# Moving work units between the turns of a transformer block: turns 0, 2, 3 and 25, and the last pair spread out

## The chip, the cores and the metric

The kernel runs on one core of one Trainium2 chip. The metric is the device time of one execution in microseconds (us). Before the change the median of three runs was 1411.21 us (1409.51 to 1415.54). A profile shows one further execution.

## The reference

The input x holds 8 batches of 512 tokens of width 256. The block computes, all in float32:

```python
x = x + attn(layernorm(x))            # attention, then a 3-tap convolution of its
                                      # context gives new queries: a second attention
                                      # with the same k and v, then out_w
x = x + ffn(layernorm(x))             # where ffn is itself:
#   h = x + attention(rmsnorm(x, g1)) # third attention, q and k rotated (rope)
#   y = h + moe(rmsnorm(h, g2))       # top 2 of 8 experts, hidden width 704
```

Each attention has 16 heads of width 16 and a causal mask. So there are three attentions for each batch, and behind them a router and a mixture of experts over all 4096 tokens.

## The kernel before, in words

**Two stages.** First come the attentions of all batches, with every projection around them; each token's normed row is written to a table in DRAM (`xtab`), grouped by expert. Then the experts run over tiles of 384 rows of that table (`expert_tile`, L814) and add their results to `out` by indirect DMA.

**Pairs and turns.** Batches are handled in pairs, called pair 0 to pair 3 here. In the code `one` and `two` are the batches of a pair, `before0` and `before1` those of the pair before it, `next0` and `next1` those of the pair after it. A pair's six attentions (first of one, first of two, second of one, and so on) have 9 steps each. A step (L1283 to L1312) is: score matmuls for 4 heads into two PSUM tiles `sc` (there are two such buffers in all), two ACT instructions `pr<-sc` that take the exponentials (L1297), and one POOL instruction that masks the diagonal (L1305). The products with the values (`av`, L1220) follow later, from a list called `behind`. Two steps make a turn, so a pair has 27 turns, numbered 0 to 26; the code writes them `t + n`.

**The order inside a turn** is written out by hand (loop at L1978): the score matmuls of the first step; the `av` products that are due; the mid slot (first `follow_up("mid")`, then `small_units`, then `first_units`); the score matmuls of the second step; `follow_up("late")`; the end slot (`units`, then `follow_up("end")`). "Mid" and "end" below mean these two slots. Engines take their instructions in exactly this order: the code is inside `tc.manual_schedule` for PE, ACT, DVE and POOL (L1898). SP, which issues most DMAs, runs in the order of the calls too.

**Units.** The other work is cut into units, methods of `Batch`, and `plan(turn, batch, method, arguments, among=...)` (L1762) puts each into a turn: `among=first_units` or `small_units` for the mid slot, else the end slot. A turn whose end slot has matmul units is in the set `busy`, and this decides how many `av` products it takes. Units that matter here: `transpose` (8 PE transposes of the normed x), `k`, `q`, `values` (projections, two halves each), `conv` (four parts), `h` (output projection of the third attention: 4 matmuls into one PSUM bank, a DVE addition L1622 into `rows`, a POOL addition, then two ACT squares L1625 that read `rows`), `rms` (normalises `rows`, stores x), `transpose3`, `logits`, `logits_back`, `route` (some 20 short DVE instructions with one ACT exponential among them), `slots` (2 matmuls and 18 short DVE instructions).

**PSUM banks.** Two banks, `mm0` and `mm1`, serve all units in turn (`mm_tile`, L1069). A unit's matmuls wait until the last reader of their bank is done.

**The ends of an attention's half.** `normalise` (L1230) copies sums on ACT, moves them by DMA, and queues `finish` (two DVE reciprocals of about 1.74 us, L1250, and two multiplications) and, for the first attention, `differences` (four DVE instructions, L1471 to L1474, that `conv` reads), to the mid slot of the next turn for the first half of the heads and to the end slot for the second half.

**The start.** `load_x(0)` fetches batch 0 in one DMA; PE runs 34 transposes of the identity meanwhile (L1906); DVE takes the moments, POOL the power, DVE the normed rows; then PE transposes them, ACT copies them out, and the first projections follow.

## Time and profile before

The profiled execution took 1413.67 us; its span, from the first to the last instruction on the core, is 1411.9 us, so 1.8 us lie around it. It is 2.46 us above the median of the three runs.

| stage (us from the span's start) | length, us | PE busy, us |
|---|---|---|
| start, 0 to 17.69 | 17.69 | 13.66 |
| pair 0, 17.69 to 224.08 | 206.39 | 201.26 |
| pair 1, 224.08 to 433.10 | 209.02 | 203.52 |
| pair 2, 433.10 to 647.85 | 214.75 | 206.79 |
| pair 3 and its end, 647.85 to 851.90 | 204.05 | 199.40 |
| rest of the experts, 851.90 to 1402.00 | 550.10 | 544.33 |
| end, 1402.00 to 1411.90 | 9.90 | 0.00 |

A turn is measured from its first score matmul to the next turn's first one. Lengths of the turns that the change touches, in us:

| turn | pair 0 | pair 1 | pair 2 | pair 3 |
|---|---|---|---|---|
| 0 | 9.43 | 8.55 | 8.55 | 8.55 |
| 2 | 6.14 | 8.98 | 8.99 | 8.48 |
| 3 | 8.74 | 8.62 | 8.86 | 8.61 |
| 4 | 9.40 | 8.82 | 8.82 | 8.82 |
| 5 | 6.23 | 7.86 | 11.92 | 5.39 |
| 6 | 6.21 | 6.79 | 6.79 | 6.28 |
| 7 | 8.44 | 8.36 | 8.36 | 8.85 |
| 10 to 14 | 34.22 | 34.88 | 34.65 | 32.32 |
| 22 to 24 | 21.50 | 21.50 | 21.49 | 24.83 |
| 25 | 9.78 | 9.77 | 9.77 | 5.90 |

Inside a turn the stretches are read the same way: from the first instruction of one group on PE to the first of the next. Where nothing delays them, the score matmuls of a step take 1.10 us (1.07 us for the steps of one block), a `k` or `q` unit 1.91 us, a `values` half 1.90 us, a `conv` part 1.92 us, an `h` half 1.92 us (1.82 us for the first of two in a row), and two transposed tiles 1.0 to 1.3 us. How to read the page: "idle before" names the instruction that ended an engine's wait; a busy PE is not PE at full rate, since score matmuls that have only one of the two `sc` buffers run two heads at a time and then take about 2.0 us for a step instead of 1.10.

### The profile page before, as it was taken

The page shows a single profiled execution, that of the slowest core. Times are in us where ns is not written, and L with a number is a line of the kernel's source. Part 1 is how long each engine was busy: PE and PEld are TensorE (multiplying, and loading weights), DVE is VectorE, ACT ScalarE, POOL GpSimd, SP SyncE. Part 2 cuts the span into 40 slices and gives each one's busy share as a digit, 9 for nine tenths or more (in the row PEclk, how much of TensorE's full clock was granted, in tenths as well). Part 3 has the DMA queues.
Part 4 walks back from the last instruction along what each step waited for, and adds up shares of the span by engine and source line. Part 5 has one row for each costly group of instructions (what it writes and reads, how often), then busy time and mean ns, then how long its engine had stood idle before and what let it go on. Part 6 is the DMA issues. An engine that isn't in the chain of part 4 may idle for free.

```text
span 1411.9 us, 31919 instructions
## 1 busy us (share of the span) xinstructions
PE 1369.0 (97%) x13476; PEld 892.3 (63%) x13476; DVE 739.6 (52%) x1470; ACT 723.6 (51%) x1175; POOL 525.2 (37%) x525
## 2 busy tenths in 40 slices
PE   8999999999999899999999999999999999999997
PEld 5566555566555566556565566666767677776775
DVE  5754886775887665886666865322222212222221
ACT  4677777776786677777776784321111211111120
POOL 3334434547333546433555444232122121222212
PEclk9999999999999999999999999999999999999998
DMA  5122122211001211011222022334141323232311
GB/s 151 59 82 86 66 82 77 73 40 62 13 25 53 73 40 55 20 45 39 83 72 79 21 84 71 90 81 102 23 102 31 96 32 95 46 87 42 88 26 14
DMA packets 66408, 88.42 MB, mean 63 GB/s; under 512 B 12752, under 2 KB 46736, under 8 KB 66256
## 3 DMA queue, kind: packets, MB, share of 16 engines
q1 hardware_dynamic: 52976, 68.94, 14.7%
q0 software_dynamic: 13280, 17.35, 7.0%
q8 instruction: 107, 1.75, 0.5%
q14 instruction: 45, 0.37, 0.1%
HBM read 36.35 MB, written 31.82 MB: 48 GB/s over the span
## 4 chain that ended last, share of the span: by engine, by line
PE 59%; DVE 5%; ACT 4%; DMA 1%; issue 1%; POOL 1%; DVEq 0%; POOLq 0%; ACTq 0%; SPq 0%
PE pgu L835 23%; PE po L860 13%; PE sc L1290 8%; PE av L1220 5%; PE mm L1130 3%; ACT pr L1297 2%; PE mm L1483 2%; PE mm L1119 1%; PE mm L1148 1%; PE mm L824 1%; DVE r L1250 1%; DVE c L1251 1%; PE mm L1372 1%; DMA r<-cs 1%; DMA cs<-cs 0%
## 5 line engine op out<-in xcount | busy, mean ns | idle before, releaser
L1297 ACT ACTIVATE pr<-sc 128x1024 f32<-128x1024 f32 x432 | 418.8, 1023 | 145.1 <-PE sc L1290 144.6
L1305 POOL TENSOR_TENSOR pr<-pr,seen 128x512 f32<-128x512 f32 (+1 forms) x216 | 256.6, 1188 | 395.7 <-ACT pr L1297 386.2
L835 PE MATMUL pgu<-xgT,gu 128*128 128x384 f32 (+1 forms) x1056 | 337.0, 478 | 1.9 <-DVE hT L850 1.6
L835 PEld LDWEIGHTS pgu<-xgT,gu 128*128 128x128 f32 x1056 | 200.4, 190 | 128.3 <-DVE hT L850 2.2
L849 ACT ACTIVATE sg<-pgu 128x384 f32<-128x384 f32 (+1 forms) x120 | 57.7, 481 | 404.5 <-PE pgu L835 404.4
L872 POOL DMA_INDIRECT out_dram<-share,xg x72 | 111.0, 1542 | 373.8 <-DVE share L867 299.6
L1220 PE MATMUL av<-pr,va 64*32 64x512 f32 (+7 forms) x6144 | 216.3, 407 | 0.0
L1290 PE MATMUL sc<-qT,kT 32*128 32x320 f32 (+7 forms) x2048 | 192.2, 436 | 4.3 <-ACT pr L1297 4.2
L850 DVE TENSOR_TENSOR hT<-sg,pgu 128x384 f32<-128x384 f32 (+1 forms) x120 | 65.0, 543 | 240.3 <-ACT sg L849 240.3
L860 PE MATMUL po<-dn,hT 128*128 128x256 f32 (+1 forms) x864 | 190.8, 379 | 0.0
L1220 PEld LDWEIGHTS av<-pr,va 64*32 64x32 f32 x6144 | 112.1, 106 | 101.2 <-issue 73.5
L860 PEld LDWEIGHTS po<-dn,hT 128*128 128x128 f32 (+1 forms) x864 | 159.9, 187 | 23.9
L1250 DVE RECIPROCAL r<-r 128x256 f32<-128x256 f32 x96 | 167.4, 1744 | 11.8 <-DMA r<-cs 11.7
L1290 PEld LDWEIGHTS sc<-qT,kT 32*128 32x128 f32 x2048 | 115.7, 185 | 78.3 <-ACT pr L1297 32.0
L867 DVE TENSOR_SCALAR share<-po,xg 128x256 f32<-128x256 f32 (+1 forms) x72 | 34.8, 483 | 148.6 <-PE po L860 148.5
L1290 PE MATMUL sc<-q2T,kT 32*128 32x512 f32 (+7 forms) x1024 | 93.0, 434 | 0.6 <-ACT pr L1297 0.5
L1730 POOL DMA_INDIRECT xtab<-rows,slot x64 | 64.0, 1000 | 46.0 <-DVE pick L1719 29.0
L1290 PEld LDWEIGHTS sc<-q2T,kT 32*128 32x128 f32 x1024 | 58.3, 184 | 32.7 <-issue 14.5
L1130 PE MATMUL mm<-xT,wqkv_sb 128*128 128x512 f32 x128 | 63.7, 624 | 3.9 <-ACT mm L1625 2.3
L1130 PE MATMUL mm<-xaT,wqkv_sb 128*128 128x512 f32 x128 | 61.3, 612 | 2.0 <-DVE xaT L1378 2.0
L1483 PE MATMUL mm<-terms,conv_sb 128*128 128x256 f32 x256 | 62.7, 390 | 0.0
L1237 ACT ACTIVATE cs<-av 128x512 f32<-128x512 f32 x96 | 56.6, 604 | 3.7 <-PE av L1220 3.2
(181 smaller groups left out, 1305.5 us busy)
## 6 DMA issues: line engine op xcount, KB each, us to landing
r<-cs SPq DMA_DIRECT2D x96, 128.0 KB, 2.0
xtab<-pad SPq DMA_DIRECT2D x24, 397.5 KB, 3.3
xg<-xtab SPq DMA_DIRECT2D x16, 397.5 KB, 3.0
gu<-in_wg_dram SPq DMA_DIRECT2D x18, 352.0 KB, 3.1
cs<-cs SPq DMA_DIRECT2D x48, 128.0 KB, 2.0
dn<-in_wd_dram SPq DMA_DIRECT2D x9, 640.0 KB, 5.1
gu<-in_wu_dram SPq DMA_DIRECT2D x18, 320.0 KB, 3.8
x<-in_x_dram SPq DMA_DIRECT2D x8, 512.0 KB, 4.3
```

The costliest lines, as they stand in the source:

```text
L835: nc.tensor.matmul(ps, gu[d][:, n0 : n0 + P], xgT[:, d, :], start=(d == 0), stop=(d == DC - 1),)
L850: nc.vector.tensor_mul(hT[k], sg, pu)
L860: nc.tensor.matmul(po, hT[k][:, s * P : s * P + m], dn[:, k, :], start=(k == 0), stop=(k == NK - 1),)
L872: nc.gpsimd.indirect_dma_start(out=out, out_offset=token_of(xg, s, m), in_=share[:m, s, :], in_offset=None, bounds_check=B * S - 1, oob_is ...
L1130: nc.tensor.matmul(ps, w[:, d, n0 : n0 + P], srcT[:, d, :S], start=(d == 0), stop=(d == DC - 1),)
L1220: nc.tensor.matmul(av[i][g * HP : (g + 1) * HP, j * KB :], v[rows, j, ch * G + g, :], pr[rows, g, at : at + n], start=(j == 0), stop=(j == ...
L1250: nc.vector.reciprocal(r[:, half], r[:, half])
L1290: nc.tensor.matmul(sc[:, g - g0, at : at + S - j * KB], kT[r0 : r0 + HP, ch, j], qT[r0 : r0 + HP, ch, j * KB : S], start=True, stop=True,)
L1297: nc.scalar.activation(pr[:, g0 : g0 + 2], sc, AF.Exp, scale=SCALE)
L1305: nc.gpsimd.tensor_tensor(diag, diag, seen.unsqueeze(1).unsqueeze(1).to_broadcast([P, G, len(parts), KB]), ALU.mult,).ins
L1483: nc.tensor.matmul(ps[:, i], conv_sb[:, d, k, ch * P : (ch + 1) * P], self.terms[d][:, k], start=(d == 0), stop=(d == DC - 1),)
L1730: nc.gpsimd.indirect_dma_start(out=xtab, out_offset=bass.IndirectOffsetOnAxis(ap=slot[:, c, k : k + 1], axis=0), in_=rows[:, c, :], in_off ...
```

## The change

Nothing is computed differently. Each unit named still runs once. The order changes in these places:

- **Start.** Batch 0 is fetched in two DMAs and its moments, powers and normed rows are taken in two halves. The bias column `bqk_sb` is fetched ahead of the weights. The bias product moves behind the normed rows. The 8 transposes go half by half into both banks, and ACT and DVE each copy one bank out. The moments of batch 1 come after that. 22 instead of 34 transposes of the identity run ahead.
- **Rope tables (pair 0).** The four `table` units move from the end of turns 3 and 4 to the mid slots of turns 2, 3, 4 and 5.
- **Turn 0.** `q 0` of batch two moves from the end slot, between the transposes and the logits, to the mid slot.
- **Turn 2.** The first `h` half moves to the mid slot, where it stands behind `route`. **Turn 3.** `slots` moves to the mid slot. **Turn 25.** The transposes of the next pair's second batch move to the mid slot.
- **Differences** always go to the end slot.
- **Squares.** The squares of `h` are written to an SBUF tile, no longer over the PSUM bank that they came from.
- **Last pair.** `q 1`, `k 1`, `values 1`, `h 1`, `rms`, `transpose3`, the `conv` parts of both batches, `slots` and `values2 0` get turns of their own, one unit to a slot, from turn 2 to turn 23. Turn 10 thereby leaves `busy`.
- **Bias additions** on POOL move to earlier turns.

```diff
--- before.py
+++ after.py
...
     xs = {}
-    def load_x(b):
+    def load_x(b, parts=1):
         if b < B:
             xs[b] = keep.tile([P, NC, D], F32, tag="x", name="x", bufs=4)
-            nc.sync.dma_start(xs[b], x[b * S : (b + 1) * S, :].rearrange("(c p) d -> p c d", p=P))
+            of = x[b * S : (b + 1) * S, :].rearrange("(c p) d -> p c d", p=P)
+            n = NC // parts
+            for c in range(0, NC, n):
+                nc.sync.dma_start(xs[b][:, c : c + n, :], of[:, c : c + n, :])
...
-    load_x(0)
+    load_x(0, 2)
...
+        bqk_sb = column(bqkv[: 2 * D], 2 * D, "bqk_sb")
         wqkv_sb = weight(wqkvT, 3 * D, "wqkv_sb")
-        bqk_sb = column(bqkv[: 2 * D], 2 * D, "bqk_sb")
...
-
         bk_sb = wp.tile([P, DC, 2], F32, tag="bk", name="bk_sb")
-        for ch in range(DC):
-            nc.vector.tensor_scalar(
-                bk_sb[:, ch, :], parity, bqk_sb[:, DC + ch : DC + ch + 1], None, ALU.mult
-            )
+
+        def bias_by_parity():
+
+            for ch in range(DC):
+                nc.vector.tensor_scalar(
+                    bk_sb[:, ch, :], parity, bqk_sb[:, DC + ch : DC + ch + 1], None, ALU.mult
+                )
...
                 for n0 in range(0, S, S // 2):
                     follow(1 - ch, lambda n0=n0: finish(n0), where)
                 if then is not None:
-                    follow(1 - ch, lambda: then(ch), where)
+                    follow(1 - ch, lambda: then(ch), "end")
                 follow(3 - 2 * ch, check, "late")
...
+            def stats(self, first=0, n=NC):
+                if first == 0:
+                    self.xb = xs.pop(self.b)
+                    self.mv = small.tile([P, NC, 2], F32, tag="mv", name="mv")
+                    self.rstd = small.tile([P, NC], F32, tag="rstd", name="rstd")
+                some = slice(first, first + n)
+                for c in range(first, first + n):
+                    moments(self.mv, self.xb, c)
+                rstd = self.rstd[:, some]
+                nc.vector.tensor_scalar(rstd, self.mv[:, some, 1], LN_EPS, None, ALU.add)
+                nc.gpsimd.tensor_tensor(rstd, rstd, neghalf[:, 0, some], ALU.pow)
...
+            def normed(self, first=0, n=NC):
+                if first == 0:
+                    self.xn = self.normed_tile("xn")
+                    self.xT = self.tile([P, DC, S], "xT", "xT")
+                xn = self.xn
+                for c in range(first, first + n):
                     nc.vector.tensor_scalar(
...
-                self.xT = self.tile([P, DC, S], "xT", "xT")
+
+            def transpose_halves(self):
+
+                ps = [mm_tile() for _ in range(DC)]
+                for half in range(2):
+                    for d in range(DC):
+                        for c in range(2 * half, 2 * half + 2):
+                            nc.tensor.transpose(
+                                ps[d][:, c * P : (c + 1) * P],
+                                self.xn[:, c, d * P : (d + 1) * P],
+                                ident,
+                            )
+                for d in range(DC):
+                    (nc.scalar.copy, nc.vector.tensor_copy)[d](self.xT[:, d, :S], ps[d])
...
                 h = self.rows[:, two, :D]
                 nc.vector.tensor_add(h, h, ps)
                 nc.gpsimd.tensor_tensor(self.xb[:, two, :], self.xb[:, two, :], h, ALU.add)
+
+                squares = small.tile([P, S], F32, tag="t1", name="t1", bufs=2)
                 for c in range(2 * half, 2 * half + 2):
                     nc.scalar.activation(
-                        ps[:, c - 2 * half], self.rows[:, c, :D], AF.Square, accum_out=self.ss[:, c : c + 1]
+                        squares[:, :D], self.rows[:, c, :D], AF.Square, accum_out=self.ss[:, c : c + 1]
                     )
...
             t = p * TURNS
             plan(t, before0, "transpose3", (0, True), (1, True))
-            plan(t, two, "q", 0)
+            plan(t, two, "q", 0, among=first_units)
             plan(t, before0, "logits")
             plan(t, next0, "stats")
             plan(t + 1, two, "values", 0)
             plan(t + 1, before0, "logits_back")
             plan(t + 2, before0, "route", among=small_units)
             plan(t + 1, before1, "normed2", 2, 3)
-            plan(t + 2, before1, "h", 0, 1)
-            plan(t + 2, before1, "rms")
-            plan(t + 3, two, "q", 1, among=first_units)
-            plan(t + 3, two, "k", 1)
-            plan(t + 3, before0, "slots")
+            plan(t + 2, before1, "h", 0, among=first_units)
+
+            last_pair = two is batches[-1]
+            if last_pair:
+                plan(t + 2, two, "q", 1)
+                plan(t + 3, two, "k", 1, among=first_units)
+                plan(t + 3, two, "values", 1)
+                plan(t + 4, before1, "h", 1)
+                plan(t + 4, before1, "rms")
+            else:
+                plan(t + 2, before1, "h", 1)
+                plan(t + 2, before1, "rms")
+                plan(t + 3, two, "q", 1, among=first_units)
+                plan(t + 3, two, "k", 1)
+            plan(t + 3, before0, "slots", among=first_units)
             plan(t + 3, next0, "fetch_next")
             plan(t + 3, next0, "normed")
-            plan(t + 4, before1, "transpose3", 0)
-            plan(t + 4, two, "values", 1)
-            plan(t + 4, before1, "transpose3", 1)
+            if last_pair:
+                plan(t + 5, before1, "transpose3", 0, 1)
+            else:
+                plan(t + 4, before1, "transpose3", 0)
+                plan(t + 4, two, "values", 1)
+                plan(t + 4, before1, "transpose3", 1)
             plan(t + 5, next0, "transpose", (0, True), (1, True), among=first_units)
             plan(t + 5, next0, "q", (0, True))
             plan(t + 6, before1, "logits")
             plan(t + 6, next0, "values", 0)
-            plan(t + 7, one, "conv", (0, 0), (0, 1))
+            if last_pair:
+                plan(t + 6, one, "conv", (0, 0))
+                plan(t + 7, one, "conv", (0, 1), among=first_units)
+            else:
+                plan(t + 7, one, "conv", (0, 0), (0, 1))
             plan(t + 7, before1, "logits_back")
             plan(t + 7, before1, "route")
             plan(t + 8, one, "conv", (1, 0))
             plan(t + 9, one, "conv", (1, 1))
             plan(t + 10, next0, "values", 1)
-            plan(t + 10, before1, "slots")
+            if last_pair:
+                plan(t + 11, before1, "slots", among=first_units)
+                plan(t + 11, two, "conv", (0, 0))
+                plan(t + 12, two, "conv", (0, 1), among=first_units)
+                plan(t + 13, two, "conv", (1, 0))
+                plan(t + 14, two, "conv", (1, 1))
+            else:
+                plan(t + 10, before1, "slots")
             plan(t + 11, next0, "k", 0)
-            for c in range(NC):
-                plan(t + 10 + c, one, "bias", c)
-                plan(t + 14 + c, two, "bias", c)
-            plan(t + 12, two, "conv", (0, 0), among=first_units)
-            plan(t + 12, two, "conv", (0, 1))
+            for c, n in enumerate((6, 8, 10, 11)):
+                plan(t + n, one, "bias", c)
+            for c, n in enumerate((10, 11, 15, 15)):
+                plan(t + n, two, "bias", c)
             plan(t + 13, next0, "k", 1)
-            plan(t + 14, two, "conv", (1, 0), among=first_units)
-            plan(t + 14, two, "conv", (1, 1))
+            if not last_pair:
+                plan(t + 12, two, "conv", (0, 0), among=first_units)
+                plan(t + 12, two, "conv", (0, 1))
+                plan(t + 14, two, "conv", (1, 0), among=first_units)
+                plan(t + 14, two, "conv", (1, 1))
...
-                plan(t + 25, next1, "transpose", (0, True), (1, True))
...
-                plan(t + 22, two, "values2", 0)
                 plan(t + 22, two, "q2", (1, False, False))
+                plan(t + 23, two, "values2", 0)
...
             units[1 + n // 2].append(lambda n=n: table_inputs(n))
-            units[3 + n // 2].append(lambda n=n: table(n))
+            small_units[2 + n].append(lambda n=n: table(n))
...
             for _ in range(2):
                 ps = mm_tile()
-                for i in range(17):
+                for i in range(11):
                     nc.tensor.transpose(ps[:, i % NC * P : (i % NC + 1) * P], ident, ident)
             one, two = batches[:2]
-            one.stats()
-            one.normed()
+            one.stats(0, 2)
+            one.stats(2, 2)
+            one.normed(0, 2)
+            one.normed(2, 2)
+            bias_by_parity()
+            one.transpose_halves()
             two.stats()
-            one.transpose(0)
-            one.transpose(1)
             one.k(0)
             one.q(0)
```

## The prediction

> **What bounds the kernel now.** I read the page's busy times first, then the waits of PE, then the timeline of single turns on PE, ACT and DVE, because a unit that moves costs or saves only in its own turn.
>
> ```profile
> PE 1369.0 (97%) x13476; PEld 892.3 (63%) x13476; DVE 739.6 (52%) x1470; ACT 723.6 (51%) x1175; POOL 525.2 (37%) x525
> PE 59%; DVE 5%; ACT 4%; DMA 1%; issue 1%; POOL 1%; DVEq 0%; POOLq 0%; ACTq 0%; SPq 0%
> ```
>
> PE sets the time, and moving units removes none of its work. Only 1411.9 - 1369.0 = 42.9 us are idle, 9.9 of them behind the last matmul. What can be won besides: score steps that run two heads at a time because ACT returns one `sc` buffer only (2.0 us instead of 1.10, counted as busy), and stretches at half clock. Turn 25 of pair 1, timeline of PE:
>
> ```profile
> 416.59 1.14 PE L1290 MATMUL sc<-qT,kT 32*128 32x512 f32 x8
> 417.66 2.44 PE L1220 MATMUL av<-pr,va 64*32 64x384 f32 x80
> 420.96 2.11 PE L1290 MATMUL sc<-qT,kT 32*128 32x448 f32 x16 [0.86 <-ACT pr L1297]
> 423.00 1.09 PE L1372 MATMUL mm<-ident,xn 128*128 128x128 f32 x8
> 424.44 1.99 PE L1119 MATMUL mm<-wo_sb,c 128*128 128x256 f32 x8 [0.35 <-DVE xT L1376]
> ```
>
> PE has nothing between 420.03 and 420.96 and then goes at half rate to 423.00, waiting for ACT; the transposes that could fill this come after it. Turn 2 of pair 1, DVE then ACT:
>
> ```profile
> 243.47 0.19 DVE L1678 TENSOR_REDUCE red<-prob 128x4 f32<-128x32 f32 x1 [0.99 <-ACT prob L1677]
> 248.70 0.16 DVE L1692 COPY rows<-token 128x4 int32<-128x4 int32 x1
> 248.77 1.27 DVE L1622 TENSOR_TENSOR rows<-rows,mm 128x512 f32<-128x512 f32 x2
> ```
>
> ```profile
> 243.22 0.22 ACT L1677 ACTIVATE prob<-prob 128x32 f32<-128x32 f32 x1
> 243.71 1.94 ACT L1297 ACTIVATE pr<-sc 128x1024 f32<-128x1024 f32 x2 [0.26 <-PE sc L1290]
> 249.49 0.39 ACT L1625 ACTIVATE mm<-rows 128x256 f32<-128x256 f32 x1 [3.84 <-DVE rows L1622]
> 251.38 1.92 ACT L1297 ACTIVATE pr<-sc 128x1024 f32<-128x1024 f32 x2
> ```
>
> `route` holds DVE until 248.8, so the additions of `h` and ACT's squares come late; the exponentials of turn 2's second step (243.71) pass before that wait. Other waits, and stretches with granted clock (the column of 1.00 and 0.50; PE busy is the second number):
>
> ```profile
> 269.37 1.06 PE L1372 MATMUL mm<-ident,xn 128*128 128x128 f32 x8 [1.60 <-DVE va L1166]
> 49.52 0.44 PE L1095 MATMUL mm<-ident,rope 128*128 128x128 f32 x2 [1.32 <-ACT kT L1419]
> 58.94 0.41 PE L1095 MATMUL mm<-ident,rope 128*128 128x128 f32 x2 [1.22 <-DVE va L1166]
> 475.60:479.00 3.40, 1.44 (x44) 0.71 (x36) 3.33 (x7) 2.96 (x6) 1.07 (x2) 1.00 0.11 40
> 479.00:482.40 3.40, 2.52 (x12) 2.11 (x16) 1.95 (x4) 0.13 (x2) 1.55 (x2) 0.50 0.32 121
> 482.40:485.80 3.40, 3.40 (x19) 1.71 (x12) 3.28 (x4) 1.84 (x2) 0.00 (x0) 0.50 0.09 34
> ```
>
> The last three are turn 5 of pair 2: PE was 42% busy, then ran at half clock for 6.8 us.
>
> **Part by part** (against the profiled execution; minus is faster).
>
> *Start, -2.1.* The first projection begins at 12.16 us, after the copy of the transposes; these begin at 10.28, because the normed rows start at 9.73, behind the bias product that waits until 9.46 for `bqk_sb`. In halves: batch 0 lands at 5.2 at the latest; moments of the second half 1.05, addition 0.2, POOL power 1.05, two rows 0.7, half the transposes 0.8, one copy 0.6 instead of two (1.07): about 9.7. That is 2.5 earlier. Batch 1 lands about 12.2 as now, its moments end at 14.6, and the eviction of `q` (15.90 now) follows at 14.6: 2.1 remain to the first score matmul. Below: -2.6; above: -0.5, if weights (issued 0.9 later) or batch 1 come late. The 12 transposes that go (0.19 us each) ran while PE waited for DVE.
>
> *Rope tables, -2.3.* The waits of 1.32 and 1.22 go, since the banks are long free in mid slots; 0.2 for more switching. Between -2.5 and -1.
>
> *Turn 25, pairs 0 to 2, -5.3.* The transposes run from 420.03 to 421.1, in ACT's shadow; the step ends by 422.7 instead of 423.0, as ACT's second exponential ends at 421.82; `h` then runs 422.7 to 424.6 instead of 424.44 to 426.36. -1.75 each. `squares` outside PSUM are needed for this: the second transposed tile takes the bank of turn 24's `h`, free at 418.9 with DVE's addition instead of 419.9. If only the 0.35 wait went, -1.
>
> *Turn 0, pairs 1 to 3, -0.3.* The step gains 0.45 (1.55 to 1.10), but `q` covered the copies of the transposes that the logits now wait for (0.7 of DVE): -0.1 each, between -0.45 and +0.4.
>
> *Turns 2 to 5, pair 1, +2.3.* `h 0`'s squares now stand on ACT ahead of the second step's exponentials, and wait for DVE's addition behind `route`. DVE has hardly a break from 232.8 on, so `route` moves with turn 0 alone: addition 248.5 to 249.15, squares to 250.1, exponentials 250.1 to 252.05 instead of 243.71 to 245.65. PE ends `h 1` at 247.0 and its next step needs the first exponential, 251.05: 4.1 us idle. Then 2.0 (one buffer at a time), 0.6 `av`, `q` 1.9, `slots` 0.5 to 256.1, the step to 257.2. Behind `h 1`'s squares (253.0), `rms` (power 1.1, rows 2.16) holds DVE until 256.6, `q`'s eviction frees the bank at 257.35, `k` ends at 259.2. Turn 3 ended at 256.70: +2.5. In turn 5 the wait of 1.60 goes, because `values`' eviction no longer stands behind four `differences` (267.83 now): +0.8 is left. The clock: the granted clock changes in steps of 3.4 us, and 4.1 idle us put at least one such span below 50% busy; 42% was followed by half clock, and 881.8 to 885.2 with 51% too, while two others with 53% were not. The 6.8 us at half clock cost 1.0 + 0.9 + 0.9 = 2.8 us (turn 5's transposes, step and `q`, against pair 1). I take 1.5 a pair, as part passes while DVE holds the bank; bounds 0.5 and 2.8.
>
> [...]
>
> *Pair 2, -2.0.* The same +0.8 and +1.5, and its turn 5 (11.92 against 7.86, of which 2.8 is clock and 1.25 a longer wait for DVE) and turn 3 (0.24 more) fall to pair 1's: -4.3.
>
> *Pair 3, turns 2 to 7, +2.3.* The addition comes at 671.9 as now, the exponentials run 673.5 to 675.4, PE is idle 3.8 to 674.5; then the step to 676.5, `av`, `k 1`, `slots`, a step and `values 1` end at 682.4, where turn 4 now begins at 679.96, with `values 1` (1.90) done instead of `h 1` (1.82). `rms` at the end of turn 4 holds DVE (squares, power 1.1, rows 2.16) ahead of both `differences`, so `conv (0,0)` in turn 6 waits about 1.5 for its terms (703.3). Turn 7 then begins at 703.8 instead of 700.46 with one `conv` part more behind it, turn 8 at 710.5 instead of 709.3: +1.2; 0.6 more if the store of x (512 KB, 3.0 us) delays the DMA `r<-cs`; clock 0.5.
>
> *Last pair, turns 10 to 14, -1.7.* Now 32.32. By the stretches (step, `av`, unit, step, `av` or unit): turn 10 1.24 + 0.45 + 2.0 + 1.1 (ACT bound, no filler), 11 2.0 + 1.94 + 0.5 + 1.15 + 1.92, 12 1.29 + 0.59 + 1.92 + 1.10 + 1.02, 13 1.5 + 2.31 + 1.07 + 1.92, 14 1.37 + 1.02 + 1.10 + 1.92: together 30.4, with 0.2 for switching 30.6. Between -3 and 0. *Turns 22 to 24, -0.9.* Turns 22 and 23 become those of pairs 0 to 2, 7.63 + 7.28; turn 24 gets 16 more `av` records: 1.32 + 2.90 + 1.18 + 3.65 = 9.05; sum 23.96 against 24.83. Between -1.5 and 0.
>
> *Queues.* The transposes, `q 0` and `table` issue no DMA; `slots`' indirect transfers are queued at the end of the turn either way; `rms` issues its store from SP as late as its additions. `h 0`'s POOL addition waits with DVE's ahead of the second step's mask, which needs the late exponentials anyway. *Nothing for* the squares' place itself, the bias additions (POOL is 37% busy) and the experts' stage: PE's work covers them; if the cover is gone, under 1 us either way.
>
> Sum: -2.1 - 2.3 - 5.3 - 0.3 + 2.3 - 2.0 + 2.3 - 1.7 - 0.9 = -10.0, so 1413.67 - 10.0 = 1403.7. The profiled execution stands 2.46 above the median 1411.21; its turn 5 of pair 2 is in the sum, so the median falls by 7.5 (0.53%).
>
> **Rivals.** *The squares do not hold the exponentials (chance 0.15).* If `route` ends earlier than I think, `h 0` only fills: turns 2 to 5 give -4.2 (turn 2 -1.0, turn 3 -1.6, turn 5 -1.6), -8.4 and -3 instead of +2.6: 1385.5; halfway 1394.6. For it: stretches of 2.27 and 1.96 in turn 2 that `h` would fill. Against: 3.84 us of ACT waiting for just this addition now. *PE gains little at turn 25 and the start (0.17):* -1 and -0.5 instead of -5.3 and -2.1: 1409.6. For it: PE is 97% busy. *Slower (0.13):* the wait behind `route` in turns 2 and 3 is not made good: 4.1 idle and 2.8 of half clock, 6.9 a pair, 20.7 instead of 2.6, while pair 2's own 4.3 stays: 1413.67 - 12.6 + 20.7 = 1421.8. It decides above 4.2 a pair against no change, 6.5 for a loss of 0.5%. Against: turn 5's wait has a DVE cause that goes. *Nothing changes (0.05):* 1411.
>
> **How the numbers follow.** The forecast has 0.50, by itself 1398 to 1409. Below 1393 lies half of the first rival, above 1412 the slower one: range 1393 to 1412. A change of 0.5% (7.06 us; about what the runs can tell from none) puts "faster" below 1404.15. Faster: 0.28 of the forecast, 0.15, 0.03 of the second rival, 0.06 for errors that favour several terms at once, taken from the forecast's slower half: 0.52. Slower: 0.13 less 0.01: 0.12. Within: 0.36.
>
> **What would show it.** ACT in turn 2: squares ahead of `pr`, with 5 to 6 us idle before them; PE: about 4 us idle at turn 3, then a clock of 0.50. Turn 25: transposes before the second step, turn about 8.0. First score matmul at 15.6. No wait at `rope`, none before turn 5's transposes. Wrong if turn 3's step follows `h 1` without a gap, or turn 25 keeps 9.8.

## The result and the profile after

The changed kernel takes 1423.67 us, median of seven runs (1419.74 to 1428.63); the kernel before, on the same chip, 1411.21 us (1409.31 to 1415.54). The ratio is 1.0086, with a 95% interval of 1.0071 to 1.0101: slower by 0.9%, where 0.5% faster was forecast. The profiled execution took 1428.63 us, the slowest of the seven and 5.0 above their median; its span is 1426.9 us, 15.0 more than the span before. So the parts told below add up to 15.0, while the medians differ by 12.5. From its page, the busy times and the shares of the chain:

```profile
PE 1381.6 (97%) x13464; PEld 898.1 (63%) x13464; DVE 741.5 (52%) x1472; ACT 723.6 (51%) x1174; POOL 525.4 (37%) x526
PE 88%; DVE 5%; ACT 3%; POOL 1%; issue 1%; DMA 1%; SPq 0%; POOLq 0%; DVEq 0%; ACTq 0%
```

Half clock means here a granted clock of 0.50 in the windows of the profile. PE has the same work but for the 12 transposes of the identity that went, and yet is busy for 12.6 us more: records are longer at half clock (the first projection below takes 6.53 us, against 3.67 at full clock in the kernel `warm34`), and where score steps go two heads at a time. Its idle time is 45.3 us against 42.9; it has moved to places where half clock follows. The timeline of the changed kernel: the start, turn 5 of pair 0, turn 2 of pair 1, turn 25 of pair 1, and turn 5 of pair 3 (columns: start, length, engine, line, what, idle time before it and who ended it):

```profile
11.44 6.53 PE L1136 MATMUL mm<-xT,wqkv_sb 128*128 128x512 f32 x8 [2.69 <-DMA wqkv_sb<-in_wqkvT_dram]
...
19.79 1.14 PE L1296 MATMUL sc<-qT,kT 32*128 32x512 f32 x8
...
62.74 0.39 ACT L1103 COPY sinT<-mm 128x256 f32<-128x256 f32 x1
63.19 0.66 PE L1378 MATMUL mm<-ident,xn 128*128 128x128 f32 x4 [1.38 <-ACT sinT L1103]
...
248.42 1.28 DVE L1647 TENSOR_TENSOR rows<-rows,mm 128x512 f32<-128x512 f32 x2
249.13 0.42 ACT L1652 ACTIVATE t<-rows 128x256 f32<-128x256 f32 x1 [5.61 <-DVE rows L1647]
250.09 1.92 ACT L1303 ACTIVATE pr<-sc 128x1024 f32<-128x1024 f32 x2
251.15 2.51 PE L1296 MATMUL sc<-qT,kT 32*128 32x448 f32 x16 [3.61 <-ACT pr L1303]
...
424.81 1.09 PE L1378 MATMUL mm<-ident,xn 128*128 128x128 f32 x8
425.84 2.00 PE L1296 MATMUL sc<-qT,kT 32*128 32x448 f32 x16
427.77 1.99 PE L1125 MATMUL mm<-wo_sb,c 128*128 128x256 f32 x8
...
698.76 2.15 DVE L1663 TENSOR_SCALAR rows<-rows,ss 128x256 f32<-128x256 f32 x4 [1.15 <-POOL ss L1660]
700.18 2.12 PE L1378 MATMUL mm<-ident,rows 128*128 128x128 f32 x8 [1.15 <-DVE rows L1663]
```

At the start of the kernel before, PE had not waited for the weights:

```profile
12.16 3.70 PE L1130 MATMUL mm<-xT,wqkv_sb 128*128 128x512 f32 x8 [0.24 <-ACT xT L1376]
```

Turn 25 fills as forecast: no gap, `h` directly behind the step. In turn 2 the chain is the one that was forecast too: the addition of `h 0` at 248.4 behind `route`, squares to 250.1, exponentials, PE idle for 3.6. What follows it is seen in the windows of the changed kernel (length, PE busy, granted clock, DMA):

```profile
245.89:249.30 3.41, 1.65 (x8) 1.00 0.00 0
249.30:252.71 3.41, 1.56 (x12) 1.00 0.00 0
252.71:256.12 3.41, 3.41 (x25) 0.50 0.34 115
256.12:259.54 3.42, 3.42 (x11) 0.50 0.43 116
```

6.8 us at half clock, in all three pairs. By turns, profiled execution against profiled execution:

| part | forecast | measured |
|---|---|---|
| start, to the first score matmul | -2.1 | +2.1 |
| rope tables (turns 2 to 5 of pair 0) | -2.3 | -0.8 (-3.1 in turns 3 and 4, +2.0 in turn 5, +0.2 in turn 2) |
| turn 25, pairs 0 to 2 | -5.3 | -4.4 |
| turn 0, pairs 1 to 3 | -0.3 | +0.1 |
| turns 2 to 5, pair 1 | +2.3 | +3.8 |
| turns 2 to 5, pair 2 | -2.0 | -0.1 |
| turns 2 to 7, pair 3 | +2.3 | +8.9 |
| turns 10 to 14, last pair | -1.7 | 0.0 |
| turns 22 to 24, last pair | -0.9 | -0.9 |
| not in the sum: turns 15 and 16, last pair | 0 | +2.7 |
| turn 8, last pair | 0 | +1.3 |
| turn 7, pairs 0 to 2; turn 15, pair 2 | 0 | +1.4; -1.6 |
| the rest of the turns; experts and end | 0 | +0.5; +2.1 |

With the +2.1 of the experts go 3.4 us more of half clock (6.8 against 3.4) in work that the change does not touch. (The parts are rounded.) Half clock inside the run is 44.4 us (6.8 at the start, 6.8, 6.8 and 17.1 in pairs 1 to 3, 6.8 in the experts), against 10.2 before (6.8 in pair 2, 3.4 in the experts).

### The profile page after: what moved, and what is told of

Its sections match the earlier page's. It is cut to its first block, busy times and chain, and to the rows that moved or that the text cites. A ratio compares the mean times of both kernels' runs of the same rounds, so it can differ in the third digit from the quotient of the medians.

```text
span 1426.9 us, 31890 instructions
## 1 busy us (share of the span) xinstructions
PE 1381.6 (97%) x13464; PEld 898.1 (63%) x13464; DVE 741.5 (52%) x1472; ACT 723.6 (51%) x1174; POOL 525.4 (37%) x526
## 4 chain that ended last, share of the span: by engine, by line
PE 88%; DVE 5%; ACT 3%; POOL 1%; issue 1%; DMA 1%; SPq 0%; POOLq 0%; DVEq 0%; ACTq 0%
PE pgu L838 23%; PE sc L1296 17%; PE av L1226 13%; PE po L863 13%; PE mm L1136 9%; PE mm L1508 4%; PE mm L1154 4%; PE mm L1125 3%; ACT pr L1303 2%; PE mm L1378 1%; PE mm L827 1%; DMA wqkv_sb<-in_wqkvT_dram 1%; POOL rstd L1560 0%; DVE xa L1565 0%; DVE r L1256 0%
## 5 line engine op out<-in xcount | busy, mean ns | idle before, releaser
L1226 PE MATMUL av<-pr,va 64*32 64x64 f32 (+7 forms) x6144 | 221.8, 410 | 0.0
L1296 PE MATMUL sc<-qT,kT 32*128 32x512 f32 (+7 forms) x2048 | 190.9, 440 | 13.0 <-ACT pr L1303 13.0
L1256 DVE RECIPROCAL r<-r 128x256 f32<-128x256 f32 x96 | 167.4, 1744 | 11.2 <-DMA r<-cs 11.1
L1296 PEld LDWEIGHTS sc<-qT,kT 32*128 32x128 f32 x2048 | 116.7, 187 | 84.0 <-ACT pr L1303 36.6
L1296 PEld LDWEIGHTS sc<-q2T,kT 32*128 32x128 f32 x1024 | 58.9, 184 | 32.0 <-issue 13.1
L1136 PE MATMUL mm<-xT,wqkv_sb 128*128 128x512 f32 x128 | 70.4, 682 | 2.7 <-DMA wqkv_sb<-in_wqkvT_dram 2.7
```

The source lines that it names most:

```text
L1136: nc.tensor.matmul(ps, w[:, d, n0 : n0 + P], srcT[:, d, :S], start=(d == 0), stop=(d == DC - 1),)
L1226: nc.tensor.matmul(av[i][g * HP : (g + 1) * HP, j * KB :], v[rows, j, ch * G + g, :], pr[rows, g, at : at + n], start=(j == 0), stop=(j == ...
L1256: nc.vector.reciprocal(r[:, half], r[:, half])
L1296: nc.tensor.matmul(sc[:, g - g0, at : at + S - j * KB], kT[r0 : r0 + HP, ch, j], qT[r0 : r0 + HP, ch, j * KB : S], start=True, stop=True,)
```

## Experiments

In the kernels below, "before" in a ratio is the kernel before on the same chip in the same session. Diffs are against the changed kernel unless another is named.

### `h 0` back, `slots` back

```diff
-            plan(t + 2, before1, "h", 0, among=first_units)
+            plan(t + 2, before1, "h", 0)
```

> The changed kernel with one line undone: `h 0` of turn 2 is issued in the end slot again, ahead of `h 1`. Theory: where `h 0` stands is the cause of the idle time at the end of turn 2 and of the half clock in turn 3. Then turn 2 of pairs 1 to 3 has under 0.5 us idle (3.6 to 4.1 now), turn 3 has no half clock (6.8 us now), and both turns together return to the lengths of the kernel before: 17.6, 17.9 and 17.1 us in pairs 1, 2, 3 instead of 22.7, 23.2 and 22.7. That is -5.1, -5.3 and -5.6: 1423.7 - 16.0 = 1407.7 (1405 to 1411). Rival one, the slower turn 3 comes from what was moved within it (`slots` in the mid slot): turn 3 keeps about 11 us and only the idle time goes, 1423.7 - 9 = 1414.7. Rival two, the half clock comes from the whole run and not from this gap: stretches of half clock stay about as long in sum (33 us in pairs 0 to 3 and at the start), the time falls by the idle time alone, about 1413.

1411.9 us, ratio 1.000 (0.998 to 1.002). Turn 2 is 8.65, 8.92 and 8.47 with 0.0 to 0.2 idle: that part of the theory holds. Turn 3 is 9.7, 11.7 and 10.3, not 8.6: between theory and rival one. The timeline of this kernel in turn 3 of pair 1 says why:

```profile
249.16 2.15 DVE L1663 TENSOR_SCALAR rows<-rows,ss 128x256 f32<-128x256 f32 x4 [1.13 <-POOL ss L1660]
251.23 0.74 DVE L1461 TENSOR_SCALAR qT<-mm,bqk_sb 128x512 f32<-128x512 f32 x1
252.03 1.99 PE L1136 MATMUL mm<-xT,wqkv_sb 128*128 128x512 f32 x4 [1.39 <-DVE qT L1461]
```

`slots` in the mid slot takes the bank that `k 1` had; `k 1` now needs the bank of `q 1`, whose eviction stands behind the rows of `rms`. In pair 2 the same wait (1.38) was followed by 6.8 us of half clock, in pair 1 by none. In pair 3 the wait is another: `values 1` waits 1.35 for ACT's eviction of `k 1`, and 3.4 us of half clock follow. So `slots` goes back too:

```diff
-            plan(t + 3, before0, "slots", among=first_units)
+            plan(t + 3, before0, "slots")
```

> The changed kernel with `h 0` of turn 2 and `slots` of turn 3 both back in the end slots. With `h 0` alone back, turn 3 still had 1.4 to 1.9 us idle, as `k 1` takes the bank of `q 1`, whose eviction on DVE stands behind the rows of `rms`. Theory: `slots` in the mid slot took the bank that `k 1` had; in the end slot, behind `k 1`, it gives it back. Idle time in turn 3 of pairs 1 to 3 is 0.9 or less (as in the kernel before), turn 3 there takes 8.6 to 8.9 instead of 9.7, 11.7 and 10.3, no half clock falls in turns 2 to 4, and the time is 1411.9 - 3 to - 5.5 = 1406.4 to 1408.9. Rival, `rms` is late by itself and `k 1` waits whatever `slots` does: turn 3 stays above 9.5, 1411 to 1413.

1407.6 us, 0.997 (0.996 to 0.998). Turn 3 is 8.6, 8.9 and 7.9 with at most 0.9 idle and no half clock. The two moves together cost the changed kernel 16 us, more than its whole loss.

### `h 0` alone

The kernel before with two edits alone:

```diff
+                squares = small.tile([P, S], F32, tag="t1", name="t1", bufs=2)
...
-                        ps[:, c - 2 * half], self.rows[:, c, :D], AF.Square, ...
+                        squares[:, :D], self.rows[:, c, :D], AF.Square, ...
...
-            plan(t + 2, before1, "h", 0, 1)
+            plan(t + 2, before1, "h", 0, among=first_units)
+            plan(t + 2, before1, "h", 1)
```

> The kernel before with two edits alone: the squares are written to SBUF instead of the PSUM bank, and `h 0` of turn 2 moves to the mid slot. Theory: this alone makes the loss. Turn 2 of pairs 1 to 3 gets about 4 us idle and turn 3 half clock, +5 each in turns 2 and 3, less what pair 2 had lost in its turn 5 (-4 if the half clock there goes): 1411.2 + 15 - 4 = 1422 (1419 to 1427). Rival, the loss needs the other moves of these turns (`slots` and `differences`) too: within 2 us of 1411.

1426.6 us, 1.0107 (1.008 to 1.013): the theory's upper half. Turn 2 gets 3.7 to 4.2 idle, turns 2 and 3 together +4.6, +4.9 and +6.4 in pairs 1 to 3. The move needs no helper to lose.

### The share of the clock

```diff
-            def project_two(self, of, w, half):
+            def project_two(self, of, w, half, times=1):
...
-                for i in range(2):
-                    project(ps[:, i], of, 2 * half + i, w, 0, D)
+                for _ in range(times):
+                    for i in range(2):
+                        project(ps[:, i], of, 2 * half + i, w, 0, D)
...
-                ps = self.project_two(self.c3, wo_sb, half)
+                times = 3 if half == 1 and self.b in (1, 3) else 1
+                ps = self.project_two(self.c3, wo_sb, half, times)
```

> The changed kernel, but in turn 2 of pairs 1 and 2 the matmuls of `h 1` are run three times into the same bank (the result is that of one), so that PE works for 3.7 us of the 4 us in which it waits for the exponentials; pair 3, which has `h 1` elsewhere, stays as it is. The rest of the order is not touched. Theory: the low share of busy PE brings the half clock, and that brings the longer turn 3. Then turn 2 keeps its length (11.6 and 12.1, at most 0.5 more, since ACT and DVE finish as before), no stretch of 0.50 follows in pairs 1 and 2, turn 3 there takes 7.0 to 8.6 instead of 11.1, and in pair 3 still 11.0 with its 6.8 us of half clock: 1423.7 - 5 to - 8 = 1415.7 to 1418.7. Rival one, turn 3 is long because ACT gives one buffer at a time and DVE is busy with `rms`: its clock is 1.00 and it takes 10 us or more, 1421 to 1424. Rival two, the clock falls whatever PE does there: turn 3 stays at 11.1, 1423 to 1425.

1419.3 us, 1.0062 (1.004 to 1.008). The windows of this kernel that answer to those above:

```profile
245.70:249.10 3.40, 3.40 (x17) 1.00 0.00 0
249.10:252.50 3.40, 3.25 (x20) 1.00 0.00 0
252.50:255.90 3.40, 3.40 (x34) 1.00 0.32 111
```

Turn 2 keeps its length (11.63 and 12.1), turn 3 falls from 11.1 to 8.8 in pairs 1 and 2, and stays at 11.2 with 6.8 us of half clock in pair 3. With the 0.2 that turn 4 gains, 6.8 us of half clock cost 2.5 us a pair here, and it did not come where PE was busy for 3.40 and 3.25 of 3.40 us (1.65 and 1.56 of 3.41 in the changed kernel): both rivals fall. (These are lengths in one profile of each kernel; the medians, 1423.67 and 1419.32, differ by 4.4 for the two pairs.) At full clock turn 3 is about as long as in the kernel before (8.62), with a wait in it that the changed kernel does not have there:

```profile
257.86 1.98 PE L1136 MATMUL mm<-xT,wqkv_sb 128*128 128x512 f32 x4 [0.80 <-DVE qT L1461]
```

So PE's work in these turns took 3.3 us longer at half clock, 0.8 of it passed in place of this wait, and 2.5 were left. Nothing of turn 2's loss is made good in turn 3.

### `route` out of the way

Base: the kernel `merged` (below). `route` moves from turn 2's mid slot to its end:

```diff
-            plan(t + 2, before0, "route", among=small_units)
...
-            plan(t + 2, before1, "h", 0)
+            plan(t + 2, before1, "h", 0, among=first_units)
...
                 plan(t + 2, before1, "h", 1)
                 plan(t + 2, before1, "rms")
+                plan(t + 2, before0, "route")
```

> The kernel `merged` with `h 0` of turn 2 in the mid slot, as in the changed kernel, but `route` moved behind `rms` to the end of turn 2. Theory: `route` on DVE is what the addition of `h 0` waits for. Then the addition follows its matmuls within 1 us, ACT's squares do not hold the second step's exponentials, PE has under 1 us idle in turn 2 of pairs 1 to 3 (3.6 to 4.1 in the changed kernel) and no half clock follows; `route` still ends ahead of `slots`. Turns 2 and 3 together take 16.5 to 17.8, the time is that of `merged` within 3 us. Rival: other work of DVE or ACT in these turns holds the squares as well: 2 to 4 us idle stay, half clock follows, and the time is 8 to 15 us above `merged`.

1417.1 us, 1.0039 (1.003 to 1.005). Turn 2 becomes the shortest of all, 7.95, without idle time: `route` was what held `h 0`. But turn 3 takes 13.1. ACT in this kernel, with PE and the rows of `rms` on DVE:

```profile
251.00 1.14 DVE L1663 TENSOR_SCALAR rows<-rows,ss 128x256 f32<-128x256 f32 x4 [1.13 <-POOL ss L1660]
252.49 0.23 ACT L1704 ACTIVATE prob<-prob 128x32 f32<-128x32 f32 x1 [3.43 <-DVE prob L1703]
252.63 1.92 ACT L1303 ACTIVATE pr<-sc 128x1024 f32<-128x1024 f32 x2
253.69 2.06 PE L1296 MATMUL sc<-qT,kT 32*128 32x384 f32 x16 [2.11 <-ACT pr L1303]
```

`route` has one ACT instruction of 0.23 us, and it waits for a DVE input behind `rms`; the exponentials of the next step stand behind it on ACT. The same wait, one turn on. In the next kernel (base `merged_new_start`) `route` stands between `h 1` and `rms`, and ACT evicts `q 1`:

```diff
-            plan(t + 2, before0, "route", among=small_units)
...
-            plan(t + 2, before1, "h", 0)
+            plan(t + 2, before1, "h", 0, among=first_units)
...
+                plan(t + 2, before0, "route")
                 plan(t + 2, before1, "rms")
-                plan(t + 3, two, "q", 1, among=first_units)
+                plan(t + 3, two, "q", (1, True), among=first_units)
```

> The kernel `merged_new_start` with `h 0` of turn 2 in the mid slot, `route` in the end slot of turn 2 between `h 1` and `rms`, and `q 1` of turn 3 evicted by ACT instead of DVE. Theory: now the additions of `h` stand ahead of `route` on DVE, the exponential of `route` on ACT follows the squares of `h 1` without a wait for `rms`, and the bank of `q 1` no longer waits for the rows of `rms`. Turn 2 of pairs 1 to 3 takes 7.9 to 8.1 as in route_behind (8.65 in `merged_new_start`), turn 3 8.0 to 8.7, no half clock in turns 2 to 4: -2 to -4 against `merged_new_start`, 1398.5 to 1400.5. Rival: the rows of `rms`, now 6 us later, hold up turn 4 (the transposes of the rows, `values 1`): a wait of 1 to 4 us in turn 4, 1402 to 1412.

1401.3 us, 0.9925 (0.991 to 0.994). Turns 2 and 3 together win 1.4 to 2.1 a pair as expected (7.95 and 7.77), but turn 5 of pairs 1 and 2 has 2.1 and 2.3 idle before its transposes, whose bank waits for the eviction of `values 1`; this stands on DVE behind both reciprocals of a `finish` (258.1 to 262.4 in pair 1). In pair 1:

```profile
263.95 1.07 PE L1378 MATMUL mm<-ident,xn 128*128 128x128 f32 x8 [2.10 <-DVE va L1172]
```

In pair 2 half clock followed. The base, `merged_new_start`, has 0.9946 (0.993 to 0.996), so the gain over it is not clear of the two intervals. The rival came about, one turn further on than it said.

### Turn 25

The kernel before, with the transposes in the mid slot, and the squares in SBUF or left in PSUM:

```diff
-                plan(t + 25, next1, "transpose", (0, True), (1, True))
+                plan(t + 25, next1, "transpose", (0, True), (1, True), among=first_units)
```

> The kernel before with two edits alone: the squares are written to SBUF, and the transposes of turn 25 move to the mid slot. Theory: turn 25 of pairs 0 to 2 takes 8.3 instead of 9.8 as in the changed kernel, and nothing is given back: 1411.2 - 4.4 = 1406.8 (1405.5 to 1408.5). Rival, turns 26 and 0 take it back, as DVE and ACT have the same work: 1411 (1409.5 to 1412.5).

> The kernel before with one edit alone: the transposes of turn 25 in the mid slot; the squares of `h` still go to the PSUM bank. As forecast (squares outside PSUM are needed): the second transposed tile waits for the squares of turn 24's `h 0`, the wait of 0.35 goes and little more, turn 25 takes 9.0 to 9.6, time 1409 to 1410.5. Rival: these squares are done when the mid slot comes, the place of the squares does not matter, turn 25 takes 8.3 to 8.4 and the time is 1406 to 1408 as with the squares in SBUF; turn 7 then also stays at 8.4 instead of the 8.8 that every kernel with the squares in SBUF shows.

With SBUF 1407.1 us, 0.9970 (0.9955 to 0.9986); with PSUM 1406.4 us, 0.9959 (0.9945 to 0.9973). Turn 25 takes 8.3 instead of 9.8 in both (7.9 once, after 0.5 more in turn 24). The move wins by itself and keeps its gain; the place of the squares does not matter. Turn 7 took 8.6 to 8.8 with PSUM too, so that side remark was wrong as well: in pairs 1 and 2 it takes 8.6 to 8.9 in nearly all kernels here, and 8.35 to 8.5 in the profile of before and in the two kernels run last. Why is open.

### The start

> The changed kernel with two lines swapped: `wqkv_sb` is asked for ahead of `bqk_sb`, as in the kernel before. Theory: the column `bqk_sb` (1024 elements of 4 bytes, one packet each) ahead of the weights makes them late; PE's wait for `wqkv_sb` (2.7 us in the changed kernel, 1.0 and 3.9 in two kernels with the same start) goes to under 0.3, the first projection begins at about 9.7 and the first score matmul at 15.3 to 16.2 instead of 19.8, if no half clock falls there. With the start 4 us shorter the time is 1423.7 - 2 to - 4 = 1419.7 to 1421.7, as the changed kernel had no half clock at the start in every execution. Rival: the weights are late because they share the DMA engines with the two halves of batch 0 and with batch 1; then the wait stays at 1 to 4 us and the time at 1422 to 1425.

The two loads swapped: 1425.1 us, 1.0097 (1.007 to 1.012), still 2.77 us of waiting for the weights, first score matmul at 18.8. The rival holds: the order of `bqk_sb` alone is not it. Then the start alone, on the kernel before:

> The kernel before with the changed kernel's start alone. In eight profiles with this start the first projection began at 9.9 to 12.5 (mean 11.2), always after a wait for the weights, and the first score matmul at 15.8 to 19.8 (mean 17.9); in four with the old start the first score matmul came at 16.6 to 17.7 (mean 17.3). Theory: the weights set the start, and half clock in half of the executions costs the rest: +0.6 on average, no difference from the kernel before that can be measured, 1411 to 1413. Rival, as forecast: the start saves 2.1, 1409.

1414.1 us, 1.0011 (1.000 to 1.002): no gain, and in its profile 3.53 of waiting and the first score matmul at 20.2. In ten profiles with 22 warm-ups PE waited 1.0 to 3.9 for the weights; half clock between 10.4 and 17.4 us came in five of them (the first projection took 5.20 to 6.53 us there, and 3.67 in the other five). The next three have the fastest plan below, with 34 warm-ups (`range(17)`); then batch 0 in one transfer (`load_x(0)`); then also the weights ahead of `bqk_sb`:

> The kernel `merged_new_start` with 34 warm-up transposes instead of 22. Theory: the low share of busy PE between 7 and 12 us comes from the transposes left out; with 34 of them PE works until about 9, the transposes of batch 0 follow and end at about 10.5, and no half clock falls before 20 us. The first projection begins at 11.3 to 12.2, since the copies are later; the first score matmul at 16.9 to 17.8 in every execution. Against `merged_new_start` (16.4 in its profile, up to 4 later in executions with half clock there) that is -1 to +1 in the median. Rival: the half clock at the start is that of the wait for the weights, and stays: first projection 12 or later, score matmul at 18 or later.

> The kernel `warm34` with batch 0 fetched in one transfer instead of two; `bqk_sb` is still asked for ahead of the weights, and the moments, rows and transposes still go in halves. Theory: the two smaller transfers ahead make the weights late; with one, PE's wait for the weights (1.57 in warm34) falls under 0.5, batch 1 lands by about 12.5 instead of 14.2, and the first score matmul comes at 15.6 to 16.8 instead of 17.3: -0.5 to -1.5 against warm34. Rival one: it is the column `bqk_sb` ahead of the weights together with the transfers' total that makes them late; the wait stays at 1 to 3 us, and the first score matmul at 17 to 18. Rival two: the later landing of batch 0 (5.2 instead of 3.8) now sets the start: no wait for the weights, first projection at 11 or later, no gain.

> The kernel `warm34` with batch 0 in one transfer and the weights asked for ahead of `bqk_sb`, so that the four loads of the start are those of the kernel before, and only the work on batch 0 (moments, rows and transposes in halves, the bias product behind the rows) is that of the changed kernel. Theory: weights at about 7.9 and batch 1 at 12.2 as in the kernel before; PE waits for the copies of the transposes alone, the first projection begins at 10.2 to 11, the first score matmul at 15.6 to 16.4 instead of 17.3: -1 to -1.7 against warm34. Rival: the weights are late here too (a wait of over 1 us), as they are in the kernel before without anyone waiting for them: first score matmul at 17 or later, no gain.

1398.5 us, 0.9905 (0.989 to 0.992), against 0.9946 (0.993 to 0.996) with 22 warm-ups; 1397.8 us, 0.9908 (0.989 to 0.992); 1396.8 us, 0.9910 (0.990 to 0.992). `warm34` won more than expected; its profile is 2.5 us shorter than that of `merged_new_start` though its start is 0.9 longer, as waits of 0.7 and 1.2 in turns 11 and 15 are missing, where nothing was changed. So not all of the 0.4% is shown to be the 12 transposes. The single executions point to the start: six of the ten of `merged_new_start` took 1400 to 1403 us and four 1408 to 1409, and none of the six of `warm34` took more than 1402.3. Only one of each has a profile, so this suggests the cause and does not show it. The three kernels are not told apart by their intervals, but their starts are: `whole_x` is as its rival one had it, `whole_x_weights` as its theory. Timelines of PE in `warm34`, then `whole_x`, then `whole_x_weights`:

```profile
8.88 1.10 PE L1427 MATMUL mm<-ident,xn 128*128 128x128 f32 x8
11.54 3.67 PE L1136 MATMUL mm<-xT,wqkv_sb 128*128 128x512 f32 x8 [1.57 <-DMA wqkv_sb<-in_wqkvT_dram]
...
17.34 1.14 PE L1296 MATMUL sc<-qT,kT 32*128 32x512 f32 x8 [0.23 <-DVE qT L1461]
```

```profile
11.21 3.67 PE L1136 MATMUL mm<-xT,wqkv_sb 128*128 128x512 f32 x8 [1.45 <-DMA wqkv_sb<-in_wqkvT_dram]
```

```profile
10.61 3.70 PE L1136 MATMUL mm<-xT,wqkv_sb 128*128 128x512 f32 x8 [0.46 <-ACT xT L1433]
...
16.13 1.14 PE L1296 MATMUL sc<-qT,kT 32*128 32x512 f32 x8
```

No half clock at the start in any of the three. The wait for the weights goes only when both edits of the loads are undone, so that they are the second transfer that SP asks for: the second half of batch 0 ahead of them, or `bqk_sb`, is enough to make PE wait (the half alone in `weights_first`, with 22 warm-ups; `bqk_sb` alone in `whole_x`). From their issue to their landing the weights took 6.1 us in the kernel before, 6.6 in `whole_x_weights`, and 9.2 in `whole_x`, where only the column of 2 KB stands between (512 elements, not 1024 as an expectation has it). How such a transfer delays them was not tried.

### The last pair, and the bias additions

> The changed kernel with the last pair planned like pairs 0 to 2 in turns 2 to 14 (`last_pair` is set to False); turns 22 to 24 keep the new order. Theory: the spreading itself costs, by `rms` ahead of the terms of `conv` in turns 4 to 8, and gains nothing in turns 10 to 14; `h 0` in turn 2 stays where it is. Turns 4 to 8 of pair 3 fall from 40.3 us to about 35.8 to 36.5, turns 10 to 14 stay at 32.3 within 0.6, and turn 16 (12.8) falls by 1 to 3, as the indirect transfers of `slots` leave POOL one turn earlier: 1423.7 - 7 = 1416.7 (1414 to 1419.5). Rival one, the half clock in turns 5 and 6 is all of it and comes again elsewhere: -2, 1421.7. Rival two, the spreading gains in turns 10 to 14 as forecast: these turns get 1.7 longer and the time falls by 4 at most.

`last_pair = False`: 1418.8 us, 1.0048 (1.003 to 1.007). Turns 4 to 8 of pair 3 fall to 36.6, turn 16 from 12.8 to 9.9. Turns 10 to 14 take 33.9, of which some 1.6 is put down to a stretch of 3.4 us at half clock: without it no gain and no loss, as in the changed kernel. The theory holds but for its size: 4.9 us were won where 7 were expected.

> The changed kernel with the bias additions of all pairs in the turns of the kernel before (10 to 13 for the first batch, 14 to 17 for the second). Theory: in turn 15 of pair 3 two additions (1.44 us) and an indirect transfer (1.0 us) stand on POOL ahead of the first power of `x1`; this makes the rows of `xa` late and gives the 1.5 us idle and 3.4 us of half clock in turn 16. With one addition a turn at most 0.5 of the idle time is left, and turn 16 of pair 3 takes 9.9 to 11 instead of 12.8. Against that, turn 15 of pair 2, which lost its wait of 1.1 us in the changed kernel, gets it back (8.0 to 9.6). Together -0.5 to -1.5: 1423.7 - 1 = 1422.7 (1421 to 1424). Rival, the indirect transfers, a turn later than in the kernel before, hold POOL by themselves: turn 16 keeps 12 us or more, and the time is 1424 to 1426.

1421.4 us, 1.0070 (1.005 to 1.009). Turn 16 of pair 3 takes 10.5, turn 15 of pair 2 is back at 9.6. POOL, DVE and PE around turn 16 of pair 3 in the changed kernel:

```profile
774.28 1.00 POOL L1757 DMA_INDIRECT xtab<-rows,slot  x1 [0.16 <-issue]
775.31 1.44 POOL L1530 TENSOR_TENSOR x<-x,outb_sb 128x256 f32<-128x256 f32 x2
776.69 1.04 POOL L1560 TENSOR_TENSOR rstd<-rstd,neghalf 128x4 f32<-128x4 f32 x1
...
774.62 0.76 DVE L1556 TENSOR_SCALAR rstd<-mv 128x2 f32<-128x2 f32 x1
775.29 0.80 DVE L1557 TENSOR_SCALAR rstd<-mv 128x2 f32<-128x2 f32 x1
...
780.25 1.09 PE L1378 MATMUL mm<-ident,xa 128*128 128x128 f32 x6 [1.06 <-DVE xa L1565]
```

The power of `x1` starts on POOL 0.6 us after its input is ready (776.09), and that input is itself late, as two small DVE instructions take 0.8 instead of 0.2. With the old places PE's wait for `xa` falls from 1.06 to 0.57 and no half clock follows (the other 0.41 of idle time in this turn stood there before the change too). So the later transfers of `slots` hold POOL too; without the spread (no transfer of `slots` there, new bias places) turn 16 has 0.4 idle as before. Each of the two is part of the cause. The new bias places take 1.6 off turn 15 of pair 2 in 11 of the 13 profiles that have them; in `h0_back` and `merged_new_start` it stays at 9.6, as in all six with the old places (9.6 to 9.8).

### What is left of the change, put together

Against the kernel before, `merged` keeps the moves named in its expectation; the one new line is

```diff
+            small_units[(2, 3, 4, 6)[n]].append(lambda n=n: table(n))
```

> What the runs so far favour, put together: of the changed kernel stay the transposes of turn 25, the squares in SBUF, `q 0` in the mid slot, `differences` in the end slot, the bias places, the order of turns 22 and 23, and the tables in mid slots, the last of them now in turn 6 instead of turn 5 (its copy on ACT came late there and cost PE 1.4 us); `h 0`, `slots`, the last pair's turns 2 to 14 and the start are as in the kernel before. If the parts add up: pair 0 -3.4 to -4, pair 1 -2.3, pair 2 -3.8 (without the half clock that the profiled execution of before had there), pair 3 -1.2, start 0: 1411.1 - 10.7 to - 11.3 = 1400 (1397 to 1403.5). Rival: the parts lean on each other (turn 15 on the spread, turn 5 on `slots`), and half of it is left: 1405 to 1408.

> The kernel `merged` with the changed kernel's start (batch 0 in halves, 22 warm-up transposes, `bqk_sb` first). In seven profiles with this start the first score matmul came at 15.8 to 19.8, on average 18.1; in three with the old start at 17.2 to 17.7. Theory: the start waits for the weights, which land at 10 to 12.5 whatever is done before, so the earlier normed rows win nothing, and the longer idle time ahead of the weights brings half clock in some executions: 0 to +2 against `merged`, 1400 to 1402. Rival, as forecast: -2 against `merged`, 1398.

`merged`: 1407.2 us, 0.9965 (0.995 to 0.998), 7 above the forecast. Turns 3 and 4 of pair 0 keep their -3.1 and turn 5 is 6.4 with the last table in turn 6, so that turns 2 to 6 win the 2.3 that was forecast for the tables; turns 0 to 25 of pair 3 take 194.8 (195.4 before). But its start was not the one of the kernel before: my edit put the bias product ahead of the moments, where DVE waited for `bqk_sb`:

```profile
8.42 0.36 DVE L1048 TENSOR_SCALAR bk_sb<-parity,bqk_sb 128x2 f32<-128x2 f32 x2 [5.02 <-DMA bqk_sb<-in_bqkv_dram]
```

This puts the first score matmul at 21.2, some 3.5 later than in the kernel before. The time lies in the rival's range, but the start puts it there, not the rival's cause. So the comparison of the two starts fell out here; `merged_new_start`, 1402.6 us, 0.9946 (0.993 to 0.996), does not have that wait. With 34 warm-ups and the old loads (`whole_x_weights`) the version is at 1396.8 us, 0.9% below the kernel before and 1.7% below the changed kernel by their ratios.

## Why the prediction was wrong

The forecast, 1403.7, had the sum -10.0; the profile shows +15.0. What would have shown it right was named, and most of it came: the squares ahead of `pr` after 5.6 us idle, about 4 us idle on PE, half clock, turn 25 near 8.0 (8.3), no wait at `rope`. The first score matmul at 15.6 did not come (19.8). Most mechanisms held; their sizes, and what was costed at nothing, did not. The 25.0 between the two sums are: pair 3's turns 2 to 7 6.6; turns 7, 8, 15 and 16, the rest of the turns and the experts, none of them in the sum, 6.3; the start 4.2; pair 2's turns 2 to 5 1.9; the last pair's turns 10 to 14 1.7; pair 1's 1.5; the tables 1.5; turn 25 0.9; turn 0 0.4. By an estimate half of it is the clock: 34 us more of half clock than before, at 2.5 us for each 6.8, are some 12.5 us, and the sum had 3.5 for new half clock and -2.8 for the old in turn 5 of pair 2.

- **Clock in turns 2 to 5** (a mis-sized term). "I take 1.5 a pair, as part passes while DVE holds the bank" was the failing step: the thrice-run `h 1` measured 2.5 a pair, near the upper bound of 2.8. A part did pass while DVE held the bank, but only 0.8 of 3.3. Without the clock, turns 2 to 4 of pair 1 cost 2.8 where 2.5 was worked out, and turn 5 gave back the 1.6 as forecast.
- **Pair 2's turn 5.** The recovery (11.92 to 6.23) came as worked out, but it was worth this only against the one profiled execution: in the four other kernels with the old order of turn 5, that turn took 7.9 three times and 12.8 once. The step "its turn 5 of pair 2 is in the sum, so the median falls by 7.5" took off 2.46 for it; in three of five profiles there was nothing like 4.3 to win, and how much of it the median of before holds was not measured.
- **Pair 3, turns 2 to 7** (+2.3, was +8.9). The step "`conv (0,0)` waits about 1.5 for its terms" looked at the wrong reader of late rows: `transpose3` in turn 5 waits first (1.15, and 0.40 for an exponential), and this brought 6.8 us of half clock in turns 5 and 6, beside the 6.8 in turn 3; for both the term had 0.5. Turn 8's +1.3 and turn 16's +2.7 were costed at nothing.
- **Last pair, turns 10 to 14** (-1.7, was 0.0). The stretches were added up as if each new slot were filled for nothing. Turns 10 to 14 were worked out as 4.8, 7.5, 5.9, 6.8 and 5.4 and took 5.3, 6.8, 6.4, 7.5 and 6.2; what turns 12 and 14 gained against before, turns 11 and 13 lost. **Turns 22 to 24** came out at -0.9 exactly.
- **Start** (-2.1, was +2.1). "Above: -0.5, if weights come late" saw the risk and took the wrong end. The weights bind in all profiles with this order of loads, and the 12 transposes, costed at nothing because they "ran while PE waited for DVE", seem to have been a cover against half clock: it came in five of ten profiles with 22 of them and in none of the three with the same work and 34, which is few. With the loads and the 34 transposes restored, the work in halves does win: the first score matmul comes at 16.1, against 16.6 to 17.7 in four profiles with the old start, 0.5 to 1.6 of the 2.1.
- **Rope tables** (-2.3, was -0.8). The two waits went (-3.1), but for the fourth table, alone in turn 5, ACT's copy stood behind two exponentials and two copies of attention sums, and the transposes waited 1.38 for their bank. "The banks are long free in mid slots" was not looked up for that turn.
- **Turn 25** (-5.3, was -4.4). Right in kind; "squares outside PSUM are needed for this" was wrong.
- **"Nothing for the bias additions (POOL is 37% busy)"** failed in turn 16, together with the spread: a mean share says nothing about the 2.4 us in front of one power. Without the spread the new places cost nothing there (9.9 in `no_spread`).

The slower rival is what came about, with 1421.8 against 1423.7, and by its own mechanism in turns 2 and 3; 0.13 was too little. That it came so close is partly luck: it had 20.7 for three pairs where turns 2 to 4 lost some 16, pair 2's own 4.3 did go, and the start, pair 3's later turns, turn 16 and the experts, which it did not have, made up the rest. Its "against" (turn 5's wait has a DVE cause that goes) was true and too small: 1.6 of about 5.3 a pair.

The busy share of PE does not foretell half clock by itself here. In the changed kernel it began behind 3.4 us with PE busy for 46% (249.30 to 252.71 above) and for 64% (696.45 to 699.86: 2.18 of 3.41), and in `h0_back` behind 71% (455.50 to 458.94: 2.43 of 3.44). Behind 48% (245.89 to 249.30 above), and in the kernel before behind 53% (267.39 to 270.80: 1.81 of 3.41), the clock stayed at 1.00. What decides it is open.

## What to carry to other kernels

Before a unit moves ahead of an exponential (or of anything PE waits for), look at each instruction that it puts on the in-order engine and at what that one's input stands behind on the next engine: an ACT instruction of 0.2 to 0.4 us held PE for 2 to 4 us where its DVE input was late, and taking it out of one turn put it into the next. Price a new wait on PE (3.61 us in the changed kernel, 1.38 in `h0_back`) with the half clock that may follow it, about 2.5 us for 6.8 us here, and price work that "fills idle time for nothing" as what it may be, the cover against that. And in a change of many small moves, weigh them one by one: of this one, several were gains (turn 25, tables, `differences`, turns 22 to 24, the first bias places), and two moves cost more than all of them won.
